# A four-layer graph network on one core: the end of layer 3 with dots as rows, its last two phases exchanged, its last single sums in two steps, and part of the output's products on GpSimd

## Chip, core and metric

The kernel runs on one core of a Trainium2 chip. The metric is the time of one execution on the device in microseconds. Engines are named as in the profile: PE is TensorE's matmul (PEld its weight load), DVE is VectorE, ACT is ScalarE, POOL is GpSimd, SP is SyncE, which here issues the loads of the adjacency matrix and the stores of the result.

## What is computed

The input is `x` (3327 nodes of 64 features) and a weighted adjacency matrix of 3327 by 3327, of which the kernel reads every block several times. Four layers follow one another, each as `x = x + layer(relu(layernorm(x)), adj)`: layer 0 is two gated steps, layer 1 a hyperbolic matrix product, layer 2 weighs the neighbours of a node by powers of one half in the order of their index, and layer 3 is a hyperbolic attention. The change is in layers 2 and 3; the reference for layer 3, cut to what matters, is

```python
left  = x_tan @ att_W[:D] + att_b ; right = x_tan @ att_W[D:]
adj_att = sigmoid(left + right.T) * adj
x_local = logmap(x[:, None, :], x[None, :, :])       # a vector for each pair of nodes
support = einsum('ij,ijd->id', adj_att, x_local)
return proj(expmap(x, support))                      # expmap ends in a mobius sum
```

Every pair of nodes needs a distance, a factor from the attention, and a weighted sum over neighbours. The last line needs, for each node, a few scalar products (of the node's features with the sum, of the sum with itself) and a single sum of the pair factors; from these some thirty small operations make two coefficients for each node, `ka` for the sum and `ch` for the node's own features `h`, and the output is `x + ka * sum + ch * h`.

## The kernel before

**Tiling.** The nodes, padded to 3328, are 26 blocks of 128. Blocks lie in 13 pairs ("columns" 0 to 12), and the columns in two groups: S (`gs_`, columns 0 to 5, 768 nodes in each half) and F (`gf`, columns 6 to 12, 896). With two halves, a full tile is 128 by 1792 numbers. `Stream` (L348) loads adjacency tiles into a limited number of places, in an order known beforehand (`uses_of_tiles`, L203), a few tiles ahead of their use.

**Layer 2** goes over the 26 sources of group F, then the 26 of S. For each, DVE makes a 0/1 `mask` (L1784), PE makes running counts of it in two accumulators, one for each half (`count`, L1815), ACT turns a count into weights (L1827), and PE applies them (`weigh`, L1837). A count goes on in the accumulator of the one before it, so it waits for ACT's reading. Beside them run two chains of node work, `support` (L1009) for F and S, which end layer 1 and make the right-hand sides of the weighing. In the first half, a small scheduler (`Weave`, L84, with `flush`, L1845) places weighings and chain steps; from source 28 on, all is in a written list, `ORDER3` (L241), from which the program is emitted name by name (L1936 and on). The list is all there is of an order: each engine takes its instructions in the order of emission.

**Layer 3** has the node work of `nodes3` (L1097; steps `n` for F and `s` for S in the list) and 13 phases (`PHASES`, L167) of seven pairs of columns each, each phase in two halves. A half has `distances` on PE, `gelus` and `square` on ACT, `tanh_d` and `tanh_t` on ACT, the product with the adjacency tile (`attention_d`, `attention_t`, L1435) on DVE, and the product of both (`factors_d`, L1453). Since distances are symmetric, off-diagonal tiles serve twice: `turned` (L1469) transposes them on PE, `factors_t` (L1476) multiplies them on DVE. Then PE sums over neighbours: `gather_d` and `gather_t` into the vector sums (L1479 through `add`) and `singles` into the single sums. A single sum's product has 32 output rows, taken from a shifted window of `p2c`, so that four of them work on four groups of 32 rows at a time. The F columns' vector sums are complete after phase 9; the last three phases lie within group S. Phase 11 is columns 4 and 5 as neighbours of 0, 1, 4 and 5, and phase 12, the last, is columns 2 to 5 of 2 and 3.

**The end.** `finish_f` (L1620, steps `f` of the list) and `finish` (L1638) do the following. `copied` takes the vector sums out of PSUM; `squares` makes the products with the node vectors and the squares; `added` (L1582) sums both over the features, with a 128 by 128 piece of the data as weights and a two-column matrix `halves` as the moving side, so that the scalar products come out with nodes on partitions (`dots`); `copied_singles` and `picked` (L1609) do the like for the single sums; `by_nodes` (L1595) transposes the vector sums. For group F all this is done within the list, for group S in `finish`. Then some 35 small DVE operations (L1656 to L1693) make `ch` and `ka`. For the output, PE adds `x` (L1701) and `ch * h` (L1705) in PSUM for blocks 12 to 25; ACT makes `ch * h` for 20 blocks, one instruction for each (L1703), and DVE for six; DVE multiplies with `ka` (`times`), adds (`plus`) and SP stores in three parts (L1714).

Of the kernel before, what the change touches and what calls it, by code (L numbers as in the profile page):

```python
# [18 lines left out]
D = 64  # L19
P = 128  # L20
# [25 lines left out]

SLOTS3, SLOTS2, SLOTS1, SLOTS01 = 4, 7, 16, 19
# [126 lines left out]
for _c in range(0, 6, 2):  # L174
# [4 lines left out]
    Phase((0, r_(0, 4)), (1, r_(1, 4))),  # L179
    Phase((0, r_(4, 6)), (1, r_(4, 6)), (4, r_(4, 6)), (5, r_(5, 6))),  # L180
    Phase((2, r_(2, 6)), (3, r_(3, 6))),
# [21 lines left out]
def uses_of_tiles():  # L203
# [9 lines left out]
    listed = sum(len(key) == 2 for key in rest)  # L213
    starts, uses = [], []
    for u in (
        FIRST + SECOND + THIRD + LAYER1,
        layer2[:NB],
        layer2[NB : len(layer2) - listed] + rest,
    ):
        starts.append(len(uses))  # L220
        uses += u
# [6 lines left out]
def order3(text):  # L228
# [14 lines left out]
    count.28.0 mask.30 count.28.1 mask.31 n n weigh.26.0 weigh.26.1 count.29.0 count.29.1 n  # L243
    n weigh.27.0 n weigh.27.1 count.30.0 count.30.1 weigh.28.0 weigh.28.1 weigh.29.0
    count.31.0 count.31.1 weigh.30.0 mask.32 mask.33 n weigh.29.1 count.32.0 mask.34
    count.32.1 weigh.30.1 weigh.31.0 count.33.0 count.33.1 mask.35 weigh.31.1 count.34.0
    count.34.1 weigh.32.0 weigh.32.1 weigh.33.0 weigh.34.0 n count.35.0 count.35.1 mask.36
    weigh.33.1 weigh.34.1 mask.37 count.36.0 weigh.35.0 count.36.1 count.37.0 n n n n n n
    weigh.36.0 weigh.35.1 mask.38 mask.39 count.37.1 mask.40 n n n count.38.0 count.38.1
    weigh.36.1 n weigh.37.0 count.39.0 weigh.37.1 mask.41 count.39.1 weigh.38.0 mask.42  # L250
    count.40.0 count.40.1 n weigh.38.1 count.41.0 weigh.39.0 weigh.39.1 weigh.40.0
    count.41.1 weigh.40.1 mask.43 count.42.0 count.42.1 n n n n weigh.41.0 weigh.41.1 n
    mask.44 mask.45 mask.46 count.43.0 count.43.1 n n n count.44.0 count.44.1 mask.47
    weigh.42.0 weigh.43.0 n n weigh.42.1 count.45.0 n n n mask.48 count.45.1 n weigh.43.1
    weigh.44.0 count.46.0 count.46.1 mask.49 weigh.44.1 count.47.0 n n n tanh_t.0.0.0
    count.47.1.1 weigh.45.0 n weigh.45.1 count.48.0 count.48.1 mask.50 weigh.46.0 mask.51
    weigh.46.1 count.49.0 weigh.47.0 tanh_t.0.0.1 tanh_t.0.1.0 count.49.1.1 weigh.47.1
    count.50.0 weigh.48.0 count.50.1.1 tanh_d.0.0 weigh.49.0 tanh_t.0.1.1 weigh.48.1
    count.51.0 count.51.1.1 weigh.49.1 distances.0.0.0 attention_t.0.0 gelus.0.0.0
    distances.0.0.1 weigh.50.0 weigh.51.0 gelus.0.0.1 attention_d.0.0 square.0.0 weigh.50.1  # L260
    weigh.51.1 wk evict distances.0.1.0 s s s tanh_t.1.0.0 gelus.0.1.0 tanh_d.0.1
    distances.1.0.0 gelus.1.0.0 distances.0.1.1 s clear.2 distances.1.0.1 gelus.0.1.1 s
    clear.1 factors_d.0.0 clear.0 square.0.1 gelus.1.0.1 gather_d.0.0 s s turned.0.0.0
    factors_t.0.0.0 distances.1.1.0 gather_t.0.0.0 turned.0.0.1 attention_t.0.1
    factors_t.0.0.1 gather_t.0.0.1 singles.0.0 s s tanh_d.1.0 turned.0.1.0 gelus.1.1.0
    factors_t.0.1.0 distances.1.1.1 s turned.0.1.1 attention_d.0.1 factors_d.0.1 square.1.0
# [151 lines left out]
def gnn_kernel(ctx: ExitStack, tc: tile.TileContext, t, out):  # L418
# [115 lines left out]
    w_second = w_l0[:, :P]  # L534
    w_l2 = w_all[:, :P]
    att = w_all[:, P : P + 4]
    b_l2, curv, attb = (w_all[:, P + 4 + i : P + 5 + i] for i in range(3))


    spares = [p0.tile([P, GROUPS[1].w], F32, name="m_t", tag=f"m_t{i}") for i in range(2)]  # L540
# [1791 lines left out]
```

## Time and profile before

| | |
|---|---|
| timed runs | 651.76 us median of three (651.25 to 652.19) |
| the profiled execution | 650.47 us, its span 648.7 us, mean granted clock 0.988 |
| PE busy | 605.6 us, 93% of the span |
| DVE busy | 450.8 us, 69% |
| ACT busy | 378.5 us, 58% |
| POOL busy | 24.4 us, 4% |
| DMA | 183 MB, mean 283 GB/s |
| layers 0 and 1 | 0 to 282 us of the span |
| layer 2 | 282 to about 413 us |
| layer 3, phases | about 409 to 628 us |
| layer 3, end | 628 to 642.7 us; the last store and the program's end follow, to 648.7 |

All views are of one execution. In the table by windows, each row is a stretch of the span in us, its length, and then the busy time of each engine with the number of its instructions, the granted clock of PE, the DMA share and the rate. In the timeline, a row is start, duration, engine, line of the kernel, operation, what is written and read, shape and count; neighbouring equal instructions are merged. A 32-bit matmul leaves two records. In the list of waits, a row is who waited for whom, with the sum, the number of times and the longest. A wait is put down to one releaser, and PE's ends are modelled.

### The profile page before, as it was taken

To read this page: it belongs to the slowest core of one execution; us is meant where nothing else is said; L and a number is where in the kernel's file an instruction comes from. 1 tells how busy PE (TensorE), PEld (TensorE's weight loads), DVE (VectorE), ACT (ScalarE), POOL (GpSimd) and SP (SyncE) were. 2 spreads that over 40 slices of the span, in tenths; PEclk is the share of its full clock that TensorE was granted. 3 is DMA by queue.
4 is the path that set the end of the run, shared out by engine and by line. 5 is a ranking of instruction groups with operands and counts; after the bars stand their busy time and mean duration, and the time that the engine had idled before them with its cause. 6 is when DMAs were issued, how large, how long until landed. Compare 5 with 4: busy or idle time off the path is not lost.

```text
span 648.7 us, 13173 instructions
## 1 busy us (share of the span) xinstructions
PE 605.6 (93%) x5584; PEld 320.5 (49%) x5584; DVE 450.8 (69%) x688; ACT 378.5 (58%) x524; POOL 24.4 (4%) x44
## 2 busy tenths in 40 slices
PE   1988999999998999889999999999999999999992
PEld 1442334334333433346666776556556555555770
DVE  3240867444588750667655867899999999999855
ACT  3111300130254510458888979999999999999614
POOL 0000000000000000020000020027000000000000
PEclk9999999999999999999999999999999999999896
DMA  8999999459997899999878877437676766766301
GB/s 336 415 397 414 377 358 347 184 180 395 419 416 324 313 416 418 418 391 339 316 250 308 341 264 272 146 106 253 210 260 205 247 223 233 232 202 221 103 2 58
DMA packets 32531, 183.41 MB, mean 283 GB/s; under 512 B 3696, under 2 KB 4752, under 8 KB 32464
## 3 DMA queue, kind: packets, MB, share of 16 engines
q1 hardware_dynamic: 32112, 181.63, 74.9%
q0 software_dynamic: 352, 0.85, 0.5%
q8 instruction: 46, 0.75, 0.5%
q14 instruction: 21, 0.17, 0.1%
HBM read 180.76 MB, written 0.85 MB: 280 GB/s over the span
## 4 chain that ended last, share of the span: by engine, by line
PE 75%; DVE 9%; DMA 7%; ACT 5%; issue 2%; POOL 1%; SPq 0%; DVEq 0%; ACTq 0%
PE bank L757 25%; PE bank L1479 16%; PE pair L1815 8%; PE bank L1837 7%; PE pair L1354 6%; DMA adj<-in_adj 6%; PE pair L1469 4%; PE pair L858 2%; ACT w L1827 2%; PE bank L1587 1%; PE pair L662 1%; DMA xn<-in_x 1%; DVE edges L485 1%; DVE d L1435 1%; PE bank L1228 1%
## 5 line engine op out<-in xcount | busy, mean ns | idle before, releaser
L757 PE MATMUL bank<-adj,m_a 128*64 128x384 f32 (+1 forms) x832 | 154.6, 518 | 9.0 <-DMA adj<-in_adj 6.5
L757 PEld LDWEIGHTS bank<-adj,m_a 128*64 128x64 f32 x832 | 56.9, 137 | 96.5 <-issue 72.4
L1827 ACT ACTIVATE w<-pair,ebias 128x896 uint16<-128x896 f32 (+1 forms) x100 | 91.3, 953 | 14.6 <-PE pair L1815 13.8
L757 PE MATMUL bank<-adj,m_b 128*64 128x384 f32 (+1 forms) x416 | 76.7, 515 | 1.3 <-ACT hm L846 1.3
L485 DVE SCALAR_TENSOR_TENSOR edges<-adj,edges 128x1792 bf16<-128x1792 f32 (+1 forms) x24 | 45.0, 1890 | 32.0 <-DMA adj<-in_adj 31.9
L1784 DVE TENSOR_SCALAR mask<-adj 128x1792 bf16<-128x1792 f32 (+1 forms) x52 | 52.1, 1028 | 15.6 <-PE pair L1815 15.4
L846 ACT ACTIVATE hm<-bank 64x384 f32<-64x384 f32 (+1 forms) x8 | 4.1, 513 | 94.3 <-DVE mh L845 94.1
L1837 PE MATMUL bank<-w,m_b 128*64 128x384 bf16 (+1 forms) x416 | 56.0, 340 | 0.0
L757 PEld LDWEIGHTS bank<-adj,m_b 128*64 128x64 f32 x416 | 28.9, 137 | 45.5 <-issue 41.6
L1354 PE MATMUL pair<-xs 64*128 64x384 f32 (+3 forms) x120 | 50.2, 501 | 0.3 <-ACT s L1370 0.2
L1354 PE MATMUL pair<-xs,xw 64*128 64x384 f32 (+3 forms) x120 | 50.2, 501 | 0.1
L1395 ACT ACTIVATE d<-leftb,righth 128x768 f32<-128x768 f32 (+3 forms) x47 | 39.1, 893 | 0.2 <-PE bank L1479 0.2
L1435 DVE SCALAR_TENSOR_TENSOR d<-d,adj 128x1792 f32<-128x1792 f32 x19 | 38.4, 2019 | 0.3 <-ACT d L1395 0.3
L1837 PE MATMUL bank<-w,h_t 128*64 128x384 bf16 x208 | 38.0, 339 | 0.0
L1815 PE MATMUL pair<-mask,tri_b 128*64 128x384 bf16 (+1 forms) x208 | 37.4, 339 | 0.0
L1815 PE MATMUL pair<-mask,rest_a 128*64 128x384 bf16 x192 | 33.5, 341 | 1.7 <-ACT w L1827 1.6
L1479 PE MATMUL bank<-d,xd 128*64 128x384 f32 (+3 forms) x236 | 33.6, 426 | 0.0
L1837 PEld LDWEIGHTS <-m_b 128*64 128x64 bf16 x416 | 25.9, 110 | 12.2 <-issue 1.0
L1476 DVE SCALAR_TENSOR_TENSOR tr<-pair,tr 128x1024 f32<-128x1024 f32 (+3 forms) x28 | 26.7, 954 | 5.2 <-PE pair L1469 4.8
L1479 PE MATMUL bank<-d,p2c 128*32 128x128 f32 (+1 forms) x348 | 29.9, 322 | 0.0
L1424 ACT ACTIVATE tr<-leftb,righth 128x512 f32<-128x512 f32 (+1 forms) x48 | 29.3, 660 | 0.0
L1815 PE MATMUL pair<-mask,tri_a 128*64 128x384 bf16 x208 | 27.6, 341 | 1.4 <-ACT w L1827 1.3
(360 smaller groups left out, 1088.3 us busy)
## 6 DMA issues: line engine op xcount, KB each, us to landing
adj<-in_adj SPq DMA_DIRECT2D x108, 896.0 KB, 6.4
adj<-in_adj SPq DMA_DIRECT2D x94, 768.0 KB, 8.5
adj<-in_adj SPq DMA_DIRECT2D x8, 640.0 KB, 4.0
adj<-in_adj SPq DMA_DIRECT2D x2, 512.0 KB, 3.6
xn<-in_x SPq DMA_DIRECT2D x3, 192.0 KB, 5.0
out<-s SPq DMA_DIRECT2D x3, 192.0 KB, 2.4
xw<-xs POOLq DMA_DIRECT2D x4, 128.0 KB, 3.2
w_l<-in_w_l SPq DMA_DIRECT2D x1, 460.0 KB, 9.7
```

Source lines behind the costliest of these rows:

```text
L485: V.scalar_tensor_tensor(e, a, 0.0, e, op0=OP.not_equal, op1=OP.add)
L757: T.matmul(acc[q][h * D : (h + 1) * D, : hi - lo], lhsT=m[:, k, :], rhs=a[:, h * g.w + lo : h * g.w + hi], start=first, stop=last,)
L1354: T.matmul(p[k][:, o : o + n], lhsT=l, rhs=r, start=not rows, stop=rows)
L1395: S.activation(columns(dirs[m, b], ph.n)[:, :, first * P : first * P + n], left_of(ph.g)[:, :, o : o + n], AF.Tanh, bias=righth[:, 2 * c + ...
L1424: S.activation(by_rows(a, m, u)[:, x : x + 2 * n].rearrange("p (b e) r c -> p b e r c", b=2), left_of(ph.s)[:, :, o : o + n * P].rearrange ...
L1435: V.scalar_tensor_tensor(a[:, :w], a[:, :w], 1.0, stream.tile(stream.now), op0=OP.add, op1=OP.mult)
L1476: V.scalar_tensor_tensor(a, p, rest_of(m), a, op0=OP.add, op1=OP.mult)
L1479: T.matmul(out, lhsT=lhsT, rhs=rhs, start=False, stop=True, skip_group_check=True)
L1784: V.tensor_scalar(masks[n][:, :w], a, 0.0, None, op0=OP.not_equal)
L1815: T.matmul(cnt[h][s * D : (s + 1) * D, P + lo : P + hi], lhsT=l, rhs=r, start=first and j == 0, stop=j == len(terms) - 1 or first and s == ...
L1827: S.activation(w, e, AF.Relu, bias=ebias)
L1837: T.matmul(acc2[i][q][h * D : (h + 1) * D, : hi - lo], lhsT=p[:, 2 * c + a, :], rhs=ws[n][:, h * g.w + lo : h * g.w + hi].bitcast(BF16), s ...
```

## The change

The list `ORDER3` is written anew from its first to its last name. It now begins with the first source of layer 2: the scheduled loop with `flush` is gone, and the two `support` chains are steps `u` and `v` of the list, so masks, counts, weighings and chain steps of layer 2's first half have a written order too. Masks keep their order of tiles. The engines' instructions in layers 2 and 3 are otherwise the same in kind and number, but their order differs in many places.

Phases 11 and 12 change places, so that the last phase is the one with columns 4 and 5. `singles` of the last half becomes two steps: step 0 clears the late accumulator and takes the turned tiles, step 1 does `picked(0)` and takes the direct tiles; in both, the four groups of 32 output rows are used in turn. `added` uses the 32-row form of the single sums: the data is the moving side, a shifted window of a zero matrix with one column of `halves` in it (`hz`, made by POOL in the place of a weight that is no longer needed) is the weights, and the results are rows (`drows`). `finish_s` (steps `e`) does columns 2, 3 and 0, 1 of group S, one product of it on POOL, so that `finish` has only columns 4 and 5; an ACT copy and two small products turn the rows into `dots`. The transposes of group F move from the list into `finish`. In the output, POOL makes `ch * h` for blocks 20 to 25 and 0 to 5, DVE as before for 6 to 11, ACT for the eight from 12 to 19; blocks 0 to 5 get their sum in PSUM like the others, and PE takes 20 to 25 first, then 0 to 5, then 12 to 19.

```diff
+    Phase((2, r_(2, 6)), (3, r_(3, 6))),
     Phase((0, r_(4, 6)), (1, r_(4, 6)), (4, r_(4, 6)), (5, r_(5, 6))),
-    Phase((2, r_(2, 6)), (3, r_(3, 6))),
...
-    def singles(m, b):
+    def singles(m, b, step=None):
...
+        sums_ = ps_ if step is None else late_
+        if step == 1:
+            picked(0)
+        if step == 0:
...
             sums_ = late_ = ends_[:, : 2 * P]
             cleared(late_)
             ds_ = ends_[:, 512:544]
-            picked(0)
-        a = columns(dirs[m, b], PHASES[m].n)
+        a = columns(dirs[m, b], PHASES[m].n) if step != 0 else None
...
+        if step is not None:
+
+            for i, (o, *one_) in enumerate(direct or turned_):
+                single(sums_, (o[0], i // 2 % 2, o[2]), *one_)
+            return
...
-    def added(g, ws_, lo, hi):
+    def added(g, ws_, r):
+        lo = (2 * r - g.c0) * P
+        n = min(2 * P, g.w - lo)
         for j, w in enumerate(ws_):
-            for i in range(lo, hi):
-                o = 32 * j + 2 * (g.c0 + i)
+            for h_ in range(2):
+                q = 32 * (2 * j + h_)
                 T.matmul(
-                    dots[:, o : o + 2],
-                    lhsT=w[:, i * P : (i + 1) * P],
-                    rhs=halves,
-                    start=True,
+                    drows[q : q + 32, :n],
+                    lhsT=hz[:, h_, ROWS - 1 - r : ROWS + 31 - r],
+                    rhs=w[:, lo : lo + n],
+                    start=(g, r) == (gf, gf.c0 // 2),
                     stop=True,
...
+    def finish_s():
+        nonlocal late_ends
+        g = gs_
+        m = p0.tile([P, GROUPS[1].w], F32, name="m_t", tag="m_t0")
+        w1, w2 = flat(big(g, "h_n")), flat(big(g, "xc"))
+        late_ends = m, w1, w2
+        for E, c in ((G, 2), (V, 0)):
+            cs = slice(c * P, (c + 2) * P)
+            S.activation(m[:, cs], x2_[:, cs], AF.Copy)
             yield
+            E.tensor_mul(w1[:, cs], xs[:, cs], m[:, cs])
+            S.activation(w2[:, cs], m[:, cs], AF.Square)
+            yield
+            added(g, (w1, w2), c // 2)
+            yield
...
     def finish():
...
+        cs = slice(4 * P, 6 * P)
+        S.activation(m[:, cs], ps_[:, 2 * P :], AF.Copy)
+        V.tensor_mul(w1[:, cs], xs[:, cs], m[:, cs])
+        S.activation(w2[:, cs], m[:, cs], AF.Square)
         copied_singles(1, late_)
-        for a, b, _ in parts_:
-            added(g, ws_, a // P, b // P)
+        added(g, (w1, w2), 2)
+        dd = flat(big(GROUPS[1], "sq"))[:, 4 * P : 6 * P]
+        S.activation(dd, drows, AF.Copy)
         picked(1)
+        v = dots.rearrange("p (j r i h) -> p i j r h", j=2, i=2, h=2)
+        for i in range(2):
+            T.matmul(
+                v[:, i],
+                lhsT=dd[:, i * P : (i + 1) * P],
+                rhs=ident.rearrange("p (j h k r) -> p j k r h", j=2, h=2, k=4)[:, :, 0],
...
+        by_nodes(gf, late_f[0], bank(3), 0, 4)
+        by_nodes(gf, late_f[0], ends_[:, 5 * P :], 4, gf.n)
         by_nodes(g, m, pair(1), 0, g.n)
...
+        sums_x.insert(1, (0, 6, bank(2)[:, : 6 * D]))
         for lo, hi, a in sums_x:
             T.matmul(a, lhsT=ident, rhs=flat(xn[:, lo:hi]), start=True, stop=False)
-        for k in [*range(12, NB), *range(6)]:
+        for lo, hi in ((20, NB), (0, 6)):
+            G.tensor_mul(w2[:, lo:hi], h[:, lo:hi], bc(ch[:, lo:hi]))
+        for k in range(12, 20):
             S.activation(w2[:, k, :], h[:, k, :], AF.Copy, scale=ch[:, k : k + 1])
...
         (_, _, a), *larger = nat[::-1]
+        V.tensor_mul(w2[:, 6:12], h[:, 6:12], bc(ch[:, 6:12]))
         times(6, 12, a[:, 6 * D :])
         plus(6, 12, xn[:, 6:12])
-        V.tensor_mul(w2[:, 6:12], h[:, 6:12], bc(ch[:, 6:12]))
         plus(6, 12, w2[:, 6:12])
         store(6, 12)
-        for lo, hi, b in larger[::-1]:
+        for lo, hi, b in larger:
             times(lo, hi, b)
         times(0, 6, a[:, : 6 * D])
-        plus(0, 6, xn[:, 0:6])
         for lo, hi, b in sums_x:
             plus(lo, hi, b.rearrange("p (k d) -> p k d", d=D))
             store(lo, hi)
-        plus(0, 6, w2[:, 0:6])
-        store(0, 6)
...
-        for n in range(len(work)):
-            mask(n + 2)
-            for part in range(2):
-                count(n, part)
-                flush(n, 2 if len(todo) > 2 * LAG + 2 else 1)
-                todo.append((n, part))
-                weave.tick()
-            if todo[0][0] == NB:
-                break
...
+        chains3 = {"u": gen_f, "v": support(gs_, m_s)}
+        STEPS3.update(mask=mask, count=count, weigh=weigh)
+        listed = iter(ORDER3)
...
+        take("l3")
...
             G.memset(p2c, 0.0)
+            G.memset(hz, 0.0)
+            for i in range(2):
+                G.tensor_copy(hz[:, i, ROWS - 1 : ROWS], halves[:, i : i + 1])
```

## The prediction

> **What bounds the kernel now.** I read the page first (TensorE, PE, is busy for 93% of the span and carries 75% of the chain that ended last), then the stages in the table by windows, then PE's waits, then the timeline of the last 45 us. All of it is one execution of 650.47 us with a span of 648.7; the three timed runs have a median of 651.76, so I work with differences and set them against that median.
>
> ```profile
> core 0: us, PE busy (x) PEld busy (x) DVE busy (x) ACT busy (x) POOL busy (x), PEclk, DMA share, GB/s
> 282.00:300.00 18.00, 16.61 (x197) 10.41 (x195) 13.99 (x20) 16.59 (x22) 0.92 (x1) 1.00 0.97 369
> 300.00:330.00 30.00, 28.62 (x330) 19.28 (x328) 23.37 (x37) 24.86 (x31) 0.00 (x0) 1.00 0.84 306
> 412.00:440.00 28.00, 25.28 (x256) 13.91 (x254) 26.75 (x34) 26.99 (x39) 4.08 (x9) 1.00 0.44 131
> 600.00:616.00 16.00, 16.00 (x155) 11.31 (x153) 13.85 (x11) 11.10 (x15) 0.00 (x0) 0.89 0.33 105
> 616.00:626.00 10.00, 10.00 (x158) 6.65 (x158) 7.24 (x8) 1.06 (x3) 0.00 (x0) 1.00 0.01 2
> 626.00:631.40 5.40, 5.40 (x62) 4.62 (x63) 1.25 (x3) 1.24 (x3) 0.00 (x0) 1.00 0.01 3
> 631.40:636.20 4.80, 2.13 (x10) 1.03 (x8) 4.12 (x33) 1.73 (x3) 0.00 (x0) 1.00 0.00 0
> 636.20:642.70 6.50, 3.36 (x4) 1.13 (x4) 5.92 (x13) 4.88 (x20) 0.00 (x0) 0.51 0.18 64
> ```
>
> First number after the stretch is its length, then PE's busy time. Layer 2's first half loses 1.39 + 1.38 = 2.8 us of PE. From 440 to 631 PE is full, and until 608 so is VectorE (DVE: 26.75 of 28 in the third row). From 631.4 a chain of small DVE operations runs alone for 4.8 us, and the output takes 6.5 us, with PE at half clock. PE's waits name two causes:
>
> ```profile
> PE pair L1815 <- ACT w L1827: 2.9, 6, 1.1
> PE bank L1479 <- DVE tr L1476: 1.6, 2, 1.1
> ```
>
> The timeline has the dots, and one group of sums twice:
>
> ```profile
> 609.40 3.21 PE L1479 MATMUL bank<-d,xd 128*64 128x256 f32 x16
> ...
> 623.94 1.74 PE L1479 MATMUL bank<-d,xd 128*64 128x256 f32 x16
> ...
> 628.02 1.05 PE L1587 MATMUL bank<-halves,h_n 128*128 128x2 f32 x8
> ...
> 631.46 0.18 DVE L1656 TENSOR_TENSOR d<-pair,qs 128x26 f32<-128x26 f32 x1 [4.18 <-PE pair L1609]
> ```
>
> The reader is to see that sixteen equal records take 1.74 us at full clock and 3.21 us at 609.4, and that a record of the dots costs 0.11 us although it streams two columns (the next group of eight starts 0.89 us later).
>
> **Dots as rows.** Removed: 26 products with two columns, 52 records: 1.88 us (606.45 to 608.33), 1.25 us (613.67 to 614.92) and 2.67 us (628.02 to 630.69), 5.80 us in all. Added: 28 products into 32 rows each, on four column groups. Four such products of 256 columns are what the single sums already are (626.38 to 626.82 in the timeline, 0.43 us a group), so six groups at 0.43 and one of 128 columns at 0.22: 2.8 us. New besides: a ScalarE (ACT) copy of the rows, nearest row L1604, 0.38 us, with about 0.12 us before and 0.05 us after it, and two products with 16 columns, nearest L1609, 0.45 us for the pair. The other half of `picked` (0.44 us) lies beside that copy, so 0.1 us of it shows. The seven transposes of `by_nodes` for the F group (614.92 to 615.92, 0.96 us as the issue goes) move behind the dots: they lie beside the DVE chain, where PE has 4.8 us and 2.1 us of work; with six transposes (0.8) and three products with x (1.67 us for two of them now, 2.1 us with the third) PE's new load there is 0.9 + 0.8 + 2.1 = 3.8 us, still covered. Without that cover they would cost 0.9. Of `finish_s`, two of three groups are taken before the last sums are ready; their copies and squares are ACT's, which has 9 us free after 616. The two-column lookup `hz` is made by GpSimd (POOL) in layer 2, where it is idle: nothing. Sum for PE: -5.8 - 0.96 + 2.8 + 0.45 + 0.1 = -3.4 us.
>
> **Phases exchanged, single sums in two steps.** The count of phases' instructions is equal; the exchange makes columns 2 and 3 final one phase earlier and lets the last phase touch 4 and 5 directly. Single sums of the last half: 14 products either way, 1.6 us, but only eight of them (0.86 us) now wait for the last factor. After the last factor (623.61) the old chain needs 7.85 us to the first small DVE operation: gather 1.74, clear 0.3, pick 0.44, singles 1.64, dots 2.67, pick 0.6, and latency. The new one: gather 1.74 + 0.25, pick 0.44, singles 0.86, three groups of rows 1.29, copy 0.55, small products 0.45, latency 0.2: 5.8. So where DVE sets the end, this part is worth 2.05 us, and the rest of the 3.4 shows only if DVE also ends earlier. It can: it idles 2.15 of 16 us in 600:616 and 0.4 before 623.6.
>
> **The clock.** 600:616 has a granted clock of 0.89: half clock from 609.05 to 612.46, after a stretch (606.2 to 609.0) of nothing but two-column products and 64-column transposes. The Trainium skill ("TensorE: Matmul & The Clock Gate", section "Why this matters for your kernels") only asks that gaps between matmul bursts stay under about 3 us. By that rule nothing was lost here, since PE was busy without a gap; by the rows 3.41 us ran at half speed, 1.7 us lost. The row decides for this execution: thin work is enough. The new products stream 256 columns and break that stretch. But the stretch is barely a window long, so I do not expect the drop in every timed run: value -0.85, ends 0 and -1.7.
>
> **Layer 2's order.** Only six waits, 2.9 us, are there to be won. A count into an accumulator has to wait until ACT has read the one before it (0.95 us, with latency 1.15). I summed PE's work between each count and its successor in the built order, with 0.75 or 0.38 us for a count and 0.49 or 0.65 for a weigh from the timeline: before, 12 places are short, by 3.2 us in all (near the 2.9 measured); after, 8, by 1.5 us. The first weigh can start near 291 instead of 294.45, because four DVE operations of `support` no longer stand behind masks (1.04 us each). So -1.7; ends -2.8 (all of it) and +1 (the burst of six weighs leaves ACT idle). DMA share is 0.97 there; tiles come in the same order, so I count nothing.
>
> **Layer 3's order.** All of it is listed anew, and no row shows the new waits. PE waits in 412:440 for 2.7 us, DVE is full, so a better order may give up to 2 us back and a worse one cost as much. Value: +0.8 against the gains, for DVE's share of them.
>
> Sum until the DVE chain starts: -3.4 - 0.85 - 1.7 + 0.8 = -5.15 us.
>
> **The output.** The chain itself (4.8 us) is unchanged. Then:
>
> ```profile
> 636.25 4.88 ACT L1703 ACTIVATE s<-h,d 128x64 f32<-128x64 f32 x20 [0.60 <-DVE d L1692]
> ...
> 638.32 3.36 PE L1705 MATMUL bank<-s,ident 128*128 128x512 f32 x4 [4.79 <-ACT s L1703]
> ...
> 642.18 0.55 DVE L1711 TENSOR_TENSOR s<-s 128x384 f32<-128x384 f32 x1
> ```
>
> DVE ends 6.5 us after the coefficient `ch` (636.22). ACT's twenty become eight, 1.95 us. DVE loses one 384-wide operation (0.55). POOL gets two products of 384 elements. How fast is POOL? The first half of layer 3 shows it:
>
> ```profile
> 440.27 0.28 POOL L1198 TENSOR_TENSOR par<-par,ab 128x48 f32<-128x48 f32 x1
> 440.73 1.22 DVE L1435 SCALAR_TENSOR_TENSOR t<-t,adj 128x1024 f32<-128x1024 f32 x1
> 440.92 1.16 POOL L1198 TENSOR_TENSOR par<-par,ab 128x48 f32<-128x48 f32 x1
> ```
>
> Twelve elements take 0.20, 48 take 0.28: 2.1 ns an element, so 0.99 us for 384. But the same operation took 1.16 while DVE ran one with two SBUF inputs, and ended as that ended. The skill ("GPSIMD Engine Reference", section "Key points") warns of contention with DVE instructions of two SBUF inputs and gives no price; taken as mild sharing, POOL would be ready at ch + 1.1 and + 2.1, and DVE would end 0.8 us earlier than now. The rows say that POOL stands still. New DVE order: mul 0.55 (two SBUF inputs), times 0.56 (PSUM: POOL runs), plus and plus 1.15 (POOL stands), then PSUM operations only. POOL's first product ends near ch + 2.85, the second near + 3.9. PE is in order behind them: at full clock 0.64, then the second from + 3.95, 0.64, then 0.86, drain 0.3, last DVE plus 0.68: + 6.4. That is 0.1 earlier than now. At half clock the three products take 4.2 us from + 2.9, and the end is + 8.1: 1.6 later. PE's idle before is now about 3.9 us; the clock fell at 636.4 after one window of 3.4 us with 0.55 us of work, so a drop needs the window to lie badly: one in three. Value -0.1, ends -0.8 and +1.6.
>
> **Total.** -5.15 - 0.1 = -5.25: 651.76 becomes 646.5.
>
> **Rivals.**
> 1. As summed: 646.5 (own range 645.0 to 647.5), chance 0.55.
> 2. POOL is held and PE is cold in the output: 1.6 more, 648.1. For it: the two L1198 rows and today's 0.51 clock. Against: PE's work now reaches later into the DVE chain. 0.25.
> 3. DVE is the bound of layer 3: its 96 to 99% from 412 to 608 speaks for it. Then only the 2.05 us behind the last factor show, and the shorter PE work turns into waiting: 649.7. Against: DVE's own idle time in 600:616. 0.13.
> 4. Slower: the new list makes DVE stand before its 50 products with turned tiles (L1476), because PE's transposes come later than planned. They wait 5.2 + 1.9 = 7.1 us today, 0.14 each. DVE is full, so all of it shows; it decides from 5.25 / 50 = 0.11 us more each. At 0.27 each the time is 653. Against: the list puts four steps between a transposition and its product where there were 3.2. 0.07.
>
> **How the numbers follow.** A measurement tells about 0.2%, 1.3 us, from no change. Cases 1 and 2 and most of 3 are faster by more: 0.88; within, the slow half of 3 and a mild 4: 0.07; slower 0.05. The range 644.6 to 650.0 takes in cases 1 to 3 and the lower ends of clock and layer 2.
>
> **What would show it.** L1587's busy time falls from 7.5 us (26 and 26 records counted with overlap) while its records are 256 wide; the small DVE chain begins 4 to 6 us earlier; the clock has no dip before it; PE's waits on L1827 near 1.5; POOL's two products last about 2.7 and 1 us; L1705 starts at ch + 2.9. I am wrong if L1476's or L1479's waits grow by more than 2 us, if the new end waits on ACT's copies, or if L1705 costs 4 us.

## The result, and the profile after

The changed kernel takes 646.9 us (median of ten runs, 644.11 to 649.88); ten runs of the kernel before have a median of 651.28. The ratio is 0.9943, with a 95% interval of 0.9924 to 0.9962: 3.7 us less, where 5.25 were predicted (the two medians by themselves are 4.4 apart). The profiled execution took 649.02 us with a span of 647.2, so it is one of the longer ones.

The same stretches by windows, with two short ones added (columns as before):

```profile
core 0: us, PE busy (x) PEld busy (x) DVE busy (x) ACT busy (x) POOL busy (x), PEclk, DMA share, GB/s
282.00:300.00 18.00, 17.24 (x197) 10.74 (x195) 13.64 (x19) 14.90 (x21) 3.32 (x5) 1.00 0.90 359
300.00:330.00 30.00, 29.85 (x340) 21.69 (x338) 23.29 (x39) 27.55 (x34) 0.00 (x0) 1.00 0.97 365
412.00:440.00 28.00, 25.63 (x242) 13.69 (x238) 26.32 (x31) 26.12 (x38) 2.23 (x5) 0.88 0.37 114
424.00:428.00 4.00, 2.96 (x32) 1.99 (x34) 3.41 (x5) 3.97 (x6) 0.00 (x0) 0.71 0.01 4
428.00:432.00 4.00, 4.00 (x40) 1.75 (x36) 3.79 (x9) 3.54 (x7) 0.38 (x1) 0.50 0.19 32
600.00:616.00 16.00, 15.96 (x224) 10.25 (x220) 15.51 (x13) 11.94 (x19) 0.95 (x1) 1.00 0.43 144
```

Layer 2's first half lost 2.8 us of PE and now loses 0.9. The clock in 600:616 is back at 1.00. But 412:440, which was at full clock, is at 0.88: PE ran at half clock for 6.8 us from 425.7. PE's waits from 281 to 626:

```profile
PE pair L1483 <- DVE tr L1490: 1.8, 2, 1.3
...
PE pair L1864 <- ACT w L1876: 0.7, 3, 0.3
...
PE bank L1493 <- ACT sq L1625: 0.5, 1, 0.5
```

The wait for ACT's weights, 2.9 us before, is 0.7. The other two lines are new. The timeline of the end:

```profile
622.72 0.38 ACT L1625 ACTIVATE sq<-bank 128x256 f32<-128x256 f32 x1 [5.30 <-PE bank L1493]
623.15 1.73 PE L1493 MATMUL bank<-d,xd 128*64 128x256 f32 x16 [0.48 <-ACT sq L1625]
...
627.87 0.62 PE L1630 MATMUL pair<-pick,sq 128*128 128x16 f32 x4
628.58 0.38 ACT L1684 ACTIVATE sq<-bank 128x256 f32<-128x256 f32 x1 [1.48 <-PE pair L1630]
629.02 0.63 PE L1688 MATMUL bank<-ident,sq 128*128 128x32 f32 x4 [0.53 <-ACT sq L1684]
...
629.96 1.15 PE L1619 MATMUL pair<-ident,m_t 128*128 128x128 f32 x9
630.58 0.18 DVE L1706 TENSOR_TENSOR d<-pair,qs 128x26 f32<-128x26 f32 x1 [4.59 <-PE pair L1619]
```

Everything between the first and the last line is one path: the last gather waits for a copy, the rows' copy (L1684) starts only when the second pick (L1630) is done, and the first operation of the DVE chain waits for transposes (L1619) that were meant to lie beside it. Last, the output:

```profile
635.37 2.02 ACT L1756 ACTIVATE s<-h,d 128x64 f32<-128x64 f32 x8 [0.60 <-DVE d L1742]
635.41 2.30 POOL L1754 TENSOR_TENSOR s<-h,d 128x384 f32<-128x384 f32 x2 [19.73 <-DVE d L1742]
...
636.67 4.33 PE L1758 MATMUL bank<-s,ident 128*128 128x384 f32 x6 [3.42 <-POOL s L1754]
...
641.03 0.69 DVE L1764 TENSOR_TENSOR s<-s,bank 128x512 f32<-128x512 f32 x1 [0.45 <-PE bank L1758]
```

POOL's two products take 1.20 and 1.14 us, PE's three are at half clock and take 4.33.

**A scale for the comparison.** In the fourteen profiles of this study layer 2 begins (its first count on PE) between 281.8 and 285.9 us: the two layers before it are the same in all kernels, and their time varies by 4 us from one execution to the next. In the profile after it begins 2.21 us later than in that of before. So I compare from there. `F` is the time from layer 2's first count to the end of DVE's last factor (`factors_d.12.1`), `E` from there to the first product of the output with `ch`, `A` their sum, and `B` the time from there to the end of DVE's last operation. "Half" is the time at half clock within `A`, with the whole us in which it begins.

From layer 2's first count on, the traces repeat closely. VectorE's instructions in `before` and `p2_output`, which are equal up to the output, start within 0.02 us of each other until the clock falls in one of them, and `e2_head` and `e4_head_tail`, which are equal up to the last factor and have no half clock there, have an `F` of 337.98 and 337.99. So a difference of some tenths between two single traces can be read, if the clock is looked at beside it.

| kernel | F, us | E, us | A, us | B, us | half, us | ratio to before (95%) |
|---|---|---|---|---|---|---|
| before | 341.29 | 12.64 | 353.93 | 6.48 | 3.4 (609) | 1 |
| after | 338.21 | 12.63 | 350.84 | 6.35 | 6.8 (425) | 0.9943 (0.9924 to 0.9962) |
| p1_layer2 | 339.09 | 12.63 | 351.72 | 6.49 | 3.4 (610) | 0.9958 (0.9940 to 0.9975) |
| p2_output | 339.59 | 13.43 | 353.03 | 5.81 | 6.8 (629) | 0.9988 (0.9973 to 1.0004) |
| p3_rows | 339.30 | 12.24 | 351.54 | 6.49 | none | 0.9964 (0.9947 to 0.9980) |
| s1_parts | 337.17 | 12.24 | 349.41 | 6.66 | none | 0.9931 (0.9907 to 0.9954) |
| e1_late_turns | 338.25 | 11.65 | 349.90 | 5.81 | 6.8 (425) | 0.9914 (0.9890 to 0.9938) |
| e2_head | 337.98 | 11.65 | 349.62 | 6.03 | none | 0.9913 (0.9885 to 0.9941) |
| e3_tail | 336.68 | 11.32 | 348.00 | 6.39 | 3.4 (424) | 0.9910 (0.9884 to 0.9936) |
| e4_head_tail | 337.99 | 11.32 | 349.31 | 5.82 | none | 0.9916 (0.9888 to 0.9944) |
| e5_fill | 339.80 | 11.64 | 351.45 | 6.16 | 3.4 (426) | 0.9954 (0.9939 to 0.9969) |
| e6_fill_tail | 339.12 | 11.32 | 350.44 | 5.82 | 6.8 (426) | 0.9936 (0.9912 to 0.9959) |
| e7_warm | 338.58 | 11.32 | 349.90 | 5.81 | none | 0.9947 (0.9927 to 0.9967) |
| e8_early | 338.95 | 11.32 | 350.28 | 6.48 | 3.4 (426) | 0.9960 (0.9943 to 0.9977) |

`F`, `E`, `A` and `B` are single executions, the ratio is of timed runs. From before to after `A` falls by 3.09, nearly all of it ahead of the last factor (`F` 3.08, `E` 0.01), `B` by 0.13, and what follows by about 0.4: 3.7 us, as much as the ratio says.

`before` and `p2_output` give the price of one window at half clock where PE has no idle time: `before` has one at 609, `p2_output` has none up to the last factor, and its `F` is 1.70 shorter, half of the 3.4 us.

My theory from the two traces: PE sets the pace; the parts gain by themselves, and a wait at the end and a half clock at 425 take some back. The rival: VectorE sets the pace from 412 on, and what PE saves ahead of the last factor is lost in waits.

### The profile page after: what moved, and what is told of

It reads as the page before. It is cut to its first block, busy times and chain, and to the rows that moved or that the text cites. A ratio compares the mean times of both kernels' runs of the same rounds, so it can differ in the third digit from the quotient of the medians.

```text
span 647.2 us, 13208 instructions
## 1 busy us (share of the span) xinstructions
PE 605.7 (94%) x5596; PEld 323.6 (50%) x5596; DVE 450.3 (70%) x686; ACT 375.8 (58%) x516; POOL 26.7 (4%) x50
## 4 chain that ended last, share of the span: by engine, by line
PE 75%; DMA 7%; DVE 7%; ACT 5%; issue 5%; POOL 0%; SPq 0%; POOLq 0%; ACTq 0%; DVEq 0%
PE bank L772 25%; PE bank L1493 16%; PE pair L1368 8%; PE bank L1886 7%; PE pair L1864 7%; DMA adj<-in_adj 6%; PE pair L1483 4%; ACT w L1876 2%; PE pair L873 2%; PE pair L677 1%; DMA xn<-in_x 1%; DVE edges L499 1%; PE bank L647 1%; PE bank L1758 1%; ACT tr L1438 0%
## 5 line engine op out<-in xcount | busy, mean ns | idle before, releaser
L1886 PE MATMUL bank<-w,h_t 128*64 128x384 bf16 (+1 forms) x208 | 38.1, 339 | 0.1
L1493 PE MATMUL bank<-d,xd 128*64 128x384 f32 (+3 forms) x236 | 32.2, 411 | 0.5 <-ACT sq L1625 0.5
L1886 PEld LDWEIGHTS <-m_b 128*64 128x64 bf16 x416 | 27.3, 110 | 10.6 <-issue 1.5
L1493 PE MATMUL bank<-d,p2c 128*32 128x128 f32 (+1 forms) x348 | 28.5, 322 | 0.0
L1864 PE MATMUL pair<-mask,tri_a 128*64 128x384 bf16 x208 | 25.8, 341 | 0.7 <-ACT w L1876 0.7
```

The costliest lines, as they stand in the source:

```text
L1493: T.matmul(out, lhsT=lhsT, rhs=rhs, start=False, stop=True, skip_group_check=True)
L1864: T.matmul(cnt[h][s * D : (s + 1) * D, P + lo : P + hi], lhsT=l, rhs=r, start=first and j == 0, stop=j == len(terms) - 1 or first and s == ...
L1886: T.matmul(acc2[i][q][h * D : (h + 1) * D, : hi - lo], lhsT=p[:, 2 * c + a, :], rhs=ws[n][:, h * g.w + lo : h * g.w + hi].bitcast(BF16), s ...
```

## The experiments

**The three parts, each alone on the kernel before.** `p1_layer2` has layer 2 up to `l3` in the new order (`FIRST2` is that part of the list), and all else as before:

```diff
-        for n in range(len(work)):
-            mask(n + 2)
...
+        for name in FIRST2.split():
+            name, *args = name.split(".")
```

> The kernel before with one part of the change alone: layer 2's first half (to source 27) in the new written order, with the u and v steps; everything after it as before. Theory A (PE sets the pace into layer 3): PE's waits for ACT's weights fall from 2.9 us to about 0.7, as they did in the changed kernel, and the time falls by about 2.2 us, to about 649.1. Theory B (VectorE is the bound of layer 3, from 412 us on it is 96 to 99% busy): the gain in layer 2 is waited for again behind it, PE idles more between 412 and 440 us, and the time stays within 0.5 us of before.

Measured: ratio 0.9958 (2.7 us less), `A` 2.21 less. PE's waits in layer 2:

```profile
PE pair L1834 <- ACT w L1846: 0.5, 2, 0.3
```

The gain is theory A's, to the tenth: what PE saves in layer 2 is not waited for again in layer 3. But this does not show which engine sets the pace there. In the trace VectorE's own instructions, too, start 2.14 us earlier from 90 us after layer 2's first count on, with the same idle times as before; a layer 3 bound by VectorE would have passed the gain on just as well.

`p2_output` changes the output alone (the output's hunks of the diff above; the sums of blocks 0 to 5 lie in the free half of the last pair).

> The kernel before with the output's part alone: the products with h on POOL for blocks 20 to 25 and 0 to 5, eight on ACT, the sums of 0 to 5 in PSUM (in a free half of the last pair of banks), and the new order on DVE and PE. Theory A (POOL is hardly held by DVE; the changed kernel had 1.26 and 1.0 us for its two products): the first L1708 product starts about 1.35 us after ch, PE at half clock needs 4.3 us for the three, and from ch to DVE's end it is 6.4 us, 0.1 less than before: time within 0.5 us of before. Theory B (as I had predicted, POOL stands while DVE reads two operands from SBUF): the first product of PE starts 2.9 us after ch, and the end comes 6.4 to 8.1 us after ch. A third case: PE is warm here, then the three products take 2.2 us and the end comes about 5 us after ch, 1.5 us less.

Measured: ratio 0.9988, its interval reaches 1. In its trace PE is at full clock in the output:

```profile
636.26 2.15 POOL L1704 TENSOR_TENSOR s<-h,d 128x384 f32<-128x384 f32 x2 [183.17 <-DVE d L1693]
...
637.37 0.91 PE L1708 MATMUL bank<-s,ident 128*128 128x384 f32 x2 [0.84 <-POOL s L1704]
```

POOL takes 1.05 and 1.14 us, though DVE runs operations with two SBUF operands beside it; PE's first product starts 1.3 us after `ch`, not 2.9. So POOL isn't held for long. `B` is 5.81, 0.67 less than before: the third case, though not as short as its 5 us. VectorE fills it almost without idle time, and one of its sums is slow. This sum of two SBUF operands (first line before, second line here) now lies beside POOL's second product:

```profile
638.07 0.56 DVE L1711 TENSOR_TENSOR s<-s 128x384 f32<-128x384 f32 x1
...
637.76 1.07 DVE L1714 TENSOR_TENSOR s<-s 128x384 f32<-128x384 f32 x1
```

It takes 1.07 us in all eleven profiles with the new output and 0.56 in the three without. So beside each other VectorE loses more than POOL; no run separates the cause. The ratio hardly shows the 0.67, and `A` here holds both the window that is missing at 609 (-1.70) and the two at 629 (`E` is 0.79 longer).

`p3_rows` has the dots as rows alone.

```diff
-            added(g, ws_, lo, min(lo + 2, g.n))
+        for r in range(g.c0 // 2, ROWS):
+            added(g, ws_, r)
...
-        by_nodes(g, m, b2, 4, g.n)
...
         V.tensor_mul(e_, ds, xq)
+        by_nodes(gf, late_f[0], ends_[:, 5 * P :], 4, gf.n)
```

> The kernel before with the dots as rows alone: 28 products into rows in the place of the 26 with two columns, the ACT copy and the two small products at the end; the last three transposes of group F stand behind the first two operations of the DVE chain. Phases, single sums, list and output as before. Theory A (PE bound at the end): PE loses 5.8 + 0.4 us and gains 3.0 + 0.6 + 0.5 us, so 2.1 us, and where the half clock at 609 goes away another 1.7: time 647.5 to 649.2. Theory B (DVE bound until its last factor): only what lies behind the last factor shows, 2.67 us of dots against 1.3 + 0.6 + 0.5: about 0.3 us, time about 651.

Measured: ratio 0.9964, `A` 2.39 less, and no half clock before the output. The timed runs fall into theory A's band, but the trace does not bear its mechanism out: by its own terms (2.1 + 1.7) `A` should be 3.8 shorter where the half clock is gone. The clock is 1.70 of the 2.39 (against `p2_output`, which has no half clock up to there either, `F` is only 0.29 shorter), so the rows by themselves are worth 0.69: 0.29 ahead of the last factor and 0.40 behind it. That is between the theories, and nearer to B's 0.3. PE has a new wait for a factor of VectorE:

```profile
PE bank L1480 <- DVE dir L1454: 0.9, 1, 0.9
```

The windows show the same (`p2_output` first, with the old dots at full clock, then `p3_rows`; columns as before):

```profile
600.00:616.00 16.00, 16.00 (x181) 11.51 (x185) 15.38 (x14) 11.82 (x16) 0.00 (x0) 1.00 0.38 123
```

```profile
600.00:616.00 16.00, 14.97 (x187) 8.94 (x187) 15.59 (x14) 12.21 (x16) 0.00 (x0) 1.00 0.38 125
```

With the old dots PE is full; with the rows PE idles for 1.03 us and VectorE is busy for 15.59 of 16. In the old order of layer 3, what the rows save here turns into waiting for VectorE.

**The waits at the end.** `e1_late_turns` edits the changed kernel:

```diff
-        by_nodes(gf, late_f[0], ends_[:, 5 * P :], 4, gf.n)
         by_nodes(g, m, pair(1), 0, g.n)
...
         V.tensor_mul(e_, ds, xq)
+        by_nodes(gf, late_f[0], ends_[:, 5 * P :], 4, gf.n)
```

> The changed kernel with one edit: the last three transposes of group F are issued behind the first two small DVE operations, not ahead of them. In the changed kernel the DVE chain starts at 630.58, 0.93 us after the two small products end, and the releaser named is the transposes' line; they write the same two banks of PSUM as the single sums that the chain's first operation reads. Theory A (the chain waits for these transposes because they write the same tile): the chain's third operation comes about 1 us earlier, the time is about 0.9 us under the changed kernel's 646.9, so about 646.0. Theory B (the chain waits for the small products or for something else): no change, and the wait is put down to another line.

```profile
627.83 0.18 DVE L1705 TENSOR_TENSOR d<-pair,qs 128x26 f32<-128x26 f32 x1 [2.63 <-PE pair L1630]
...
628.99 0.18 DVE L1709 TENSOR_TENSOR d<-bank,Bq 128x26 f32<-128x26 f32 x1 [0.89 <-PE bank L1688]
```

Ratio 0.9914, `A` 0.94 less than after, as theory A has it (the intervals of the two ratios overlap, so it is the trace that shows it). The chain's first two operations now follow the second pick, the third the small products. The three transposes write another part of the tile that the first operation reads (columns from 640 on, where it reads 512 to 537), and they had been issued ahead of it: that made it wait. Both parts lie in the same half of a tile of two PSUM banks; whether the tile or the bank decides was not tried.

`e3_tail` adds three small moves:

```diff
-    gather_t.12.1.1 singles.12.1.0 factors_d.12.1 singles.12.0 gather_d.12.1
+    gather_t.12.1.1 singles.12.0 factors_d.12.1 singles.12.1.0 gather_d.12.1
...
-        dd = flat(big(GROUPS[1], "sq"))[:, 4 * P : 6 * P]
+        dd = sq_[:, 4 * P : 6 * P]
-        picked(1)
...
+        by_nodes(gf, late_f[0], bank(3), 0, 4)
...
-        by_nodes(gf, late_f[0], bank(3), 0, 4)
+        picked(1)
...
+        V.tensor_mul(su, ss, Bq2)
         V.tensor_mul(b_, ds, qs)
```

> The kernel with the last three transposes of F late, and three small moves behind the last factor: the single sums of phase 12's first half go ahead of step 0 of its second half (so that ACT's copy of the first single sums is done when the last gather starts, which waited 0.48 us for it); the rows' copy gets a part of the buffer that the single sums' copies lie in, not the buffer anew (in the changed kernel it waited until the second pick had read that buffer); and the second pick follows the two small products, with the chain's third operation first. Theory A (these waits lie on the path): 0.5 + 0.4 us less from the last factor to ch, time about 644.6. Theory B (the end is set by PE's sum of work alone, or by the late transposes): less than 0.3 us.

```profile
618.97 0.38 ACT L1628 ACTIVATE sq<-bank 128x256 f32<-128x256 f32 x1 [4.63 <-PE bank L1495]
619.86 1.73 PE L1495 MATMUL bank<-d,xd 128*64 128x256 f32 x16
...
624.72 0.38 ACT L1687 ACTIVATE sq<-bank 128x256 f32<-128x256 f32 x1 [0.91 <-PE bank L1610]
...
625.62 0.60 PE L1633 MATMUL pair<-pick,sq 128*128 128x16 f32 x4
```

The waits are gone: the last gather follows without idle time, and the rows' copy starts behind the rows (L1610), ahead of the second pick. In the changed kernel `dd` asked for the buffer `sq` anew, in which the copies of the single sums lay that the second pick reads. `A` is 1.90 under `e1_late_turns`, but only 0.33 of it is in `E`; 1.57 are in `F`, gained just behind the place where the clock fell, and this execution had one window at half clock in the place of two. The timed ratios (0.9910 and 0.9914) don't tell the two kernels apart. So the end's waits are worth 0.33 us in the trace, and the timed runs don't show it.

**The parts together, without the new layer 3.** `s1_parts` is the three edits of `p1`, `p2` and `p3` in one kernel.

> The kernel before with the three parts together that were run alone: layer 2's first half in the new order, the dots as rows, and POOL in the output. The phases, the single sums and the list from layer 3 on stay as before. Alone they were 0.42, 0.36 and 0.12% faster. Theory A (PE sets the pace, the parts add up): 0.9% faster, about 645 us, so more than the whole change brought (0.57%), and the rest of the change, that is the new order of layer 3 with the exchanged phases and the single sums in two steps, is what gives it back. Theory B (what one part frees, VectorE's work takes up; the parts overlap): 0.5 to 0.6% faster, about 647.5, like the whole change, and the new order of layer 3 costs nothing.

Measured: ratio 0.9931; `A` is 4.52 less, and `p1` and `p3` alone make 2.21 + 2.39 = 4.60 (in both sums 1.70 is the clock at 609). They add up in the traces. By the timed runs the result lies between the theories (0.9907 to 0.9954 holds both 0.9910 and 0.9945). Against it the whole change is 1.43 us longer in `A`: 1.04 in `F`, with 6.8 us of half clock in it, and 0.39 in `E`. The early transposes are 0.94 of the 1.43. The new list from layer 3 on, the exchanged phases and the two steps so cost 0.5 us in that trace.

**The start of layer 3.** `e2_head` is `e1_late_turns` with the old order from `distances.0.0.0` to phase 3.

> The kernel of the run before with the last three transposes of F late, and layer 3's first part, from its first distances to the start of phase 3, in the order of the kernel before; layer 2 and all later phases in the new order. Theory A (the new order's start of layer 3 costs: three transpositions in a row wait for VectorE between 423 and 425.4, and the clock falls to half for two windows, 6.8 us, behind it): no half clock near 425, and 1 to 1.7 us less from the start of layer 2 to the coefficient ch, time about 644.3 (0.991 falls to about 0.989 of before). Theory B (VectorE was the bound there and went on working, so PE's half clock was covered): no change, 645.5.

No half clock near 425, as theory A has it, but only 0.28 us less in `A`, and the same ratio. Neither theory: the old order by itself costs about as much as two windows at half clock cost the new one. (`e3_tail`, the new order with one window, reaches the last factor 1.30 us sooner than this.) `e4_head_tail` is `e2_head` with the moves of `e3_tail`.

> Both together: the head of layer 3 in the old order and the three small moves at the end. Theory A: the gains add up, 1.9 to 2.6 us under the run with late transposes alone, so 643 to 643.6, 1.1 to 1.2% faster than before. Theory B: as for the two alone, no more than 0.3 us.

Ratio 0.9916: the gains don't add up. `A` is 349.31, 0.31 less than `e2_head`, all of it in `E` (so the moves are worth 0.3 here too), and 1.31 more than `e3_tail`, all of it in `F`.

Three kernels were to take the half clock away by giving PE work where it waits. In the changed kernel it waits here:

```profile
422.54 0.66 PE L1483 MATMUL pair<-ident,sq 64*128 64x64 f32 x16
424.52 0.34 PE L1483 MATMUL pair<-ident,sq 64*128 64x64 f32 x4 [1.32 <-DVE tr L1490]
425.38 0.92 PE L1483 MATMUL pair<-ident,sq 64*128 64x64 f32 x16 [0.52 <-DVE tr L1490]
```

`e5_fill` moves `gelus.1.1.0 distances.1.1.1` ahead of `turned.0.0.1`; `e6_fill_tail` does so in `e3_tail`; `e7_warm` is `e6_fill_tail` with the output's products of `x` made twice; `e8_early` is `e3_tail` with another order (here and above, the list's line breaks are left out):

```diff
-    gather_d.0.0 s s distances.1.1.0 turned.0.0.0 factors_t.0.0.0 turned.0.0.1 factors_t.0.0.1 turned.0.1.0
+    gather_d.0.0 turned.0.0.0 factors_t.0.0.0 distances.1.1.0 turned.0.0.1 factors_t.0.0.1 turned.0.1.0 s s
```

> The kernel with the last three transposes of F late, and one more move in the list: gelus.1.1.0 and distances.1.1.1 go ahead of turned.0.0.1, so that PE has about 1 us of work in the 1.3 us in which it waited for VectorE there. Two traces with the new order (the changed kernel and the one with late transposes) had two windows at half clock from 425, a third (with the small moves at the end) one window, and that one was 1.56 us shorter from the start of layer 2 to the last factor. Theory A (the idle 1.84 us of 3.4 in that window is what drops the clock, and PE is the bound, so each window costs 1.7 us): no half clock near 425, 1.7 to 3.4 us less from layer 2's start to ch than the 349.9 of the run with late transposes, time 642.5 to 644. Theory B (the window is covered by VectorE's work): no change, 645.5.

> The same move together with the three small moves behind the last factor. Theory A: 0.9 us less than the run with the fill alone, about 642 to 643, 1.3% faster than before. Theory B: as the run with the small moves at the end, 645.4.

> As the run before, with the three products of x in the output made twice (the first time for nothing), so that PE has 2.2 us more work beside the chain of small DVE operations. Theory A (PE's idle time beside the chain is what drops the clock in the output; at half clock the three last products take 4.3 us and the output 6.4, at full clock 2.2 to 2.7 and 5.8): the output is 5.8 us in the trace, and the time 0.2 to 0.5 us under the run before. Theory B (POOL and DVE set the output's end, not PE): the output stays at about 5.8 to 6.4 as it falls, no difference in time.

> The kernel with late transposes and the three small moves at the end, and, in place of the fill that had no ready work, another move at the start of layer 3: turned.0.0.0 goes ahead of distances.1.1.0, so that these products (whose buffers were free) lie in the gap, and two steps s (two VectorE operations of about 1 us that stood before the first product with turned tiles) go behind turned.0.1.0. Theory A (PE's idle time in that window drops the clock, and PE is the bound): PE idles at most 0.7 us between 421 and 425.7, no half clock near 425, and 1.7 us less from layer 2's start to ch than the 348.0 of the run with the small moves, which had one such window: 346.3, time about 644. Theory B (VectorE is the bound there): 348 as before the move, time 645.4. If the clock falls all the same, idle time isn't what drops it.

`e5_fill` and `e8_early` were slower than what they start from (0.9954 and 0.9960 against 0.9914 and 0.9910), `e6_fill_tail` 0.9936, `e7_warm` 0.9947. The first line is `e5_fill`'s, the second `e7_warm`'s, the last two are `e8_early`'s:

```profile
426.39 0.84 PE L1370 MATMUL pair<-xs,xw 64*128 64x384 f32 x1 [2.53 <-ACT s L1386]
```

```profile
424.33 0.59 PE L1370 MATMUL pair<-xs,xw 64*128 64x384 f32 x1 [2.53 <-ACT s L1386]
```

```profile
423.31 0.84 ACT L1128 ACTIVATE sq<-xc 128x768 f32<-128x768 f32 x1 [2.78 <-DVE xc L1126]
...
425.85 0.67 PE L1370 MATMUL pair<-xs,xw 64*128 64x384 f32 x1 [3.32 <-ACT s L1386]
```

The products that `e5_fill` to `e7_warm` move were not ready: their place in PSUM comes free when ACT has read the pair before, and ACT is 93% busy there (26.12 of 28 us after). PE stood for ACT in the place of VectorE, and for longer. In `e8_early` the moved products ran at once, but the two steps `s` that went behind them made ACT stand for VectorE (L1128), and so the next distances came later still.

The clock fell in `e5_fill`, `e6_fill_tail` and `e8_early`. In `e7_warm`, whose order up to the output is that of `e6_fill_tail`, it did not fall. So these three traces give prices in one and the same order: against `e7_warm` at full clock, `F` is 0.54 longer with 6.8 us at half clock (`e6_fill_tail`) and 1.22 longer with 3.4 us (`e5_fill`). And the gain of theory A does not come even at full clock, since the fill itself costs: `e7_warm` needs 1.90 us more in `F` than `e3_tail` with a window at half. What this stretch takes at full clock in the changed kernel's own order stays open. As for `e7_warm`'s output, `B` is 5.81, but 5.82 in `e6_fill_tail`, whose clock did not fall there either; the times don't differ. That run tells nothing of the output.

## Why the prediction was right, and where it was not

**Layer 2: right, a little small.** -1.7 was predicted, `p1_layer2` shows -2.21. The count of short gaps (3.2 to 1.5 us) was a fair guide; the waits that are left are 0.7.

**Dots as rows: right in PE's work, too large in time.** The rows take 1.54 us for F (612.88 to 614.42) and 1.60 for S (626.27 to 627.87), 3.1 in the place of 5.8; 2.8 were predicted. But the prediction counted PE's whole saving of 3.4 as time saved, and alone, in the old order, the rows are worth 0.69 beside the clock (`p3_rows`). The reason given for counting it in full, VectorE's 2.15 us of idle time in 600:616, was for the most part the half clock itself: in `p2_output`, with the same dots at full clock, VectorE idles for only 0.62 us there. In the changed kernel PE is full there (15.96 of 16), but its order is new too, so the term can't be read from it alone.

**The clock: right.** The eleven profiles with rows have no half clock between 600 us and the chain of small operations, and the three with two-column products have it before that chain, from 609, 610 and 629. The Trainium skill's rule ("TensorE: Matmul & The Clock Gate", section "Why this matters for your kernels") about gaps was no guide here: in the 3.4 us before each of these three falls PE had no idle time at all. That thin products are the reason is what the change of form suggests; column counts in between were not tried. In 112 runs of the kernel before, those with a mean granted clock of 0.985 and less have a median of 652.3, of 0.987 and 0.988 651.1, of 0.990 and more 649.9: a window of 3.4 us (0.0026 of the mean) goes with about 1.2 us; the two traces above give 1.70 for the one at 609, so 0.85, which allowed for runs without the fall, was low for this pair of traces.

**The step that failed** is "they lie beside the DVE chain" (the F group's transposes), and with it the 5.8 us from the last factor to the chain. It took 7.83 (622.75 to 630.58), as much as before (7.85), so that none of the 2.05 us forecast behind the last factor came. Term by term: the last gather starts 0.40 late, because the exchanged phases put its sums into the bank that ACT's copy of the single sums reads; the rows 1.60 for 1.29; the second pick's 0.71 stands ahead of the rows' copy and not beside it; and 1.09 pass from the small products to the chain, for transposes that I had at nothing, with 0.9 named as the price without cover. These four are 2.5 us over the forecast; shorter terms elsewhere give back 0.5. `e1_late_turns` took 0.98 off `E`, and `e3_tail` another 0.33. Two of the prediction's own signs of being wrong came true here and in the output: the new end waits on ACT's copies (0.48 and 0.53), and the output's products cost over 4 us (4.33). I had looked at engines and not at tiles: who writes a tile ahead of its reader.

**Layer 3's order: +0.8 was near by luck.** The term was meant for new waits, and the half clock near 425 was not in it. Against `s1_parts` the new order is +1.04 in `F`, with two windows at half clock; `e3_tail`, with one, is 0.49 under `s1_parts`. So the order itself is not the slower one; the clock takes its gain. What a window costs near 425 has no single value: 1.57 from `e1_late_turns` to `e3_tail` with one window less, but 0.54 for two and 1.22 for one in the order of the fill. In ten timed runs of the changed kernel the four at a mean clock of 0.990 have a median of 648.9, the six above 646.3; these 2.6 us are more than one window's 1.7, so the clock near 425 is not all of the difference.

**The output: right by two errors.** -0.1 was predicted and -0.13 measured, but POOL is ready at ch + 1.3 and + 2.4, not + 2.85 and + 3.9, and PE was at half clock, which I had given +1.6. That the two cancel is luck. `B` is 6.16 to 6.66 in the five profiles with the new output in which the clock falls within 2.4 us behind `ch`, and 5.81 to 6.03 in the six in which it falls later or not at all; the old output, at half clock in all three of its profiles, has 6.48 and 6.49. So the new one gains up to 0.7 if PE keeps its clock and nothing if it doesn't; the old one at full clock was not seen.

**The rivals.** The third case, VectorE as the bound with a gain only behind the last factor, did not come: the changed kernel gains 3.08 us ahead of it and 0.01 behind. `p1_layer2` does not decide between the engines. In the old order VectorE does take over in 600:616 once PE's dots are shorter (`p3_rows`). The slower case did not come: VectorE's waits before products with turned tiles fell from 6.6 to 5.5 us in that line's own view. The median, 646.9, falls into the first case; the ratio's 3.7 us, taken from 651.76, make 648.1, where the second case stands, but its mechanism (POOL held by DVE) is not what happened. What was lost against the sum are 2.0 us net behind the last factor and the clock near 425; what was won are 0.5 us more in layer 2 and, in this trace, 0.85 more from the clock at 609.

## What to carry to other kernels

Work that is moved beside a chain is free only if no instruction of the chain reads the tile it writes, or takes a buffer whose reader stands behind it: look for tile and buffer, not for the engine's idle time. Before filling a gap of PE, ask whether the work to be put there has its place in PSUM free at that time; with ACT and VectorE nearly full, a gap can move and grow. A gain that comes through a later stage does not show which engine bounds that stage, if the other engines' work moves with it. Idle time that was read at half clock is no reserve for the kernel at full clock. And compare executions from a common mark when an earlier stage varies by more than the effect.

## What the runs showed of the hardware

PE's clock fell for two windows of 3.4 us after one window in which PE was idle for 1.84 us of it, in gaps of 1.32 and 0.52, none near the length of a window (after and `e1_late_turns`; one window in `e3_tail`, with the same gaps). Idle time of that size did not always lower it: in the profile after, PE was idle for 1.86 of the 3.41 us from 84.36, and the clock stayed at 1.00. How the idle time falls on the windows matters: counted in steps of 3.41 us from each trace's own change of clock, `e6_fill_tail` was idle for 2.50 us of the window from 423.05 and its clock fell; `e7_warm`, with the same order, was idle for 1.52 and 1.53 of the windows from 419.91 and 423.32, and its clock stayed. So one order can run with and without the fall. What is counted within a window stays open.

One window at half clock cost 1.70 us where PE was full (at 609), and between 0.5 and 1.6 near 425, for one or two windows.

POOL's products of 384 elements took 1.05 to 1.20 us beside DVE operations with two SBUF operands, where the slope of the small ones gives 0.99 and the prediction's full hold 2.7; DVE's sum beside the second product took 1.07 in the place of 0.56. What held POOL in the profile of before were operations of another kind (scalar_tensor_tensor on 1024 and more elements); whether the kind makes the difference was not tried.
